# Layers 2 and 3 of a conv-attention kernel: from two streams ordered by a planner to four blocks in one written order

## The chip, the cores and the metric

The kernel runs on one core of one Trainium2 chip. The metric is the device time of one execution in microseconds (us). TensorE is called PE here (PEld is its weight loading), VectorE DVE, ScalarE ACT, GpSimd POOL and SyncE SP.

## The reference

An input of 8 images with 128 channels and 16x16 positions (256 tokens an image, 2048 in all) goes through four layers, all in float32:

- Layer 0: an "adder" convolution (sums of absolute differences) with residual.
- Layer 1: three selective scans (Mamba branches), a channel attention, two 3x3 convolutions.
- Layer 2: attention and a mixture of experts, for each image:
```python
x = x + softmax(LN(x Wq) @ LN(x Wk).T / sqrt(D)) @ (x Wv)      # x normed first
p = softmax(LN(x) @ router_w + router_b)                       # 8 experts, best 2 kept, renormed
x = x + sum_e p_e * (LN(x) @ expert_w[e] + expert_b[e])
```
- Layer 3: an encoder-decoder of eight Performer layers (linear attention over 8 heads with 44 random features), each followed by an MLP of 512 hidden units with GELU, and a bottleneck of 10 units after the fourth; then a spectral layer:
```python
h = LN(x) @ tok_W + pos
for i in range(8):
    u = LN(h); q, k, v = rotary(u Wq), rotary(u Wk), u Wv
    kf = exp(k F - |k|^2/2 - max) + eps; qf = exp(q F - |q|^2/2 - max) + eps
    h = h + (qf @ (kf.T @ v) / (qf @ sum(kf))) @ Wo
    h = h + gelu(LN(h) @ W1) @ W2
    if i == 3: h = gelu(h @ enc) @ dec
x = x + tanh(h);  out = x + spectral(LN(x))
```

## The kernel before

The 2048 tokens are four blocks of 512 columns (two images each); a block's activations are tiles of 128 channels by 512 tokens. Layers 0 and 1 and the spectral layer are not changed. `mamba_layer` (layer 1) ends with convolutions on PE, named `conv` in the profile; its last two pairs of images are finished there, so X of blocks 2 and 3 is ready last.

`performer_layer` holds layers 2 and 3. It makes two streams, `_performer_stream`, one for blocks 0 and 1 and one for blocks 2 and 3. Each stream has its own pools: `ptwo` (two buffers for each name), `pmany` (five buffers shared by short-lived tiles) and `pps`, four of the eight PSUM banks. Within a stream two blocks go side by side: `_norms` does both blocks' layer norms (`xc` on PE, square on ACT, `var` on PE, logarithm and exponential on ACT, `u` on DVE), `_layer2` the attention of each image (`_image`) and the experts, `_performer_attention` one Performer attention.

A stream is a generator that yields between parts; `interleave` takes one part of each stream in turn. That is the order in which the instructions are recorded, and not yet the order in which the engines run them: a planner with costs of its own then orders each engine's queue by priority and by when it thinks the inputs are ready. The first `HALF_LAYER` = 16 parts of the first stream are recorded with the priority of layer 1's last convolutions.

ACT needs its function table reloaded when it goes from exponentials and logarithms (`LN_EXP`) to GELU and tanh (`GELU`) or back; the class `Tables` holds the activations of each stretch of one stream between its two loads, and the two streams cross each other. Loads appear in the profile as `ACT_TABLE_LOAD`.

Weights of one Performer layer (`lw`, 948 KB) are loaded by SP in `_Layer`, with two buffers in the pool `plw`, one load for both streams; the first use of a layer makes it.

Names that the profile shows in one Performer layer, in the order of the computation: `xc`, `var`, `u` (norm); `pa`, `ro`, `rk`, `rq`, `sqk`, `sqq` (k and q with the rotation; `rk` and `rq` end on POOL); `pl`, `dt`, `dg` (squares by head, transposed); `pf`, `mxk`, `ek` (features of k, for each of four groups of 128 tokens); `m`, `pm`, `gm`, `dm`, `pg` (maximum over all tokens of an image); `pv`, `vo` (values); `pq`, `mq`, `ex`, `px`, `qp` (features of q, transposed); `pc`, `ctx`, `ks` (k by v); `pn`, `rd`, `po` (result, H); then `xc`, `var`, `u`, `p<-u,lw` and `g` (hidden units with GELU), `p<-g,lw` (back to 128), H. In layer 2 the router is `pl<-lw,u`, the routing a chain of small operations on the tile `ex`, and the experts `pe` on PE and `y` on DVE (line 1160), ended by `po2e`. The spectral layer begins with `p<-T,H`, which needs `pt` (line 1626) of its images.

Before the change the queues of PE, DVE, ACT and POOL in layer 1's scans are already written by hand with `tc.manual_schedule`, which makes the recorded order the order of those four engines.

Of the kernel before, what the change touches and what calls it, by code (L numbers as in the profile page):

```python
# [16 lines left out]
P = 128  # L17
# [248 lines left out]


class Tables:

    def __init__(self, E):
        self.E = E
        self.at = len(E.nc.cur_bb.bb.instructions)
        self.last = None

    def use(self, name):
        ins = self.E.nc.scalar.preload_act_table_set(name).ins
        traced = self.E.nc.cur_bb.bb.instructions
        for i in traced[self.at :]:  # L280
            if i is ins or i.engine != ins.engine:
                continue
            self._order(ins, i)
            if self.last is not None:
                self._order(i, self.last)
        if self.last is not None:
            self._order(ins, self.last)
        self.at, self.last = len(traced), ins

    def _order(self, late, early):  # L290
        info = mybir.DependencyInfo(mybir.DependencyClass.NoSync, mybir.DependencyReason.DATA)
        self.E.tc.add_manual_dep(late, early.name, info, reason="tables")
# [727 lines left out]

class _Layer2:
# [44 lines left out]

def _layer2(S, x):

    nc, two, many = S.nc, S.two, S.many
# [3 lines left out]
    us = yield from _norms(S, x)  # L1073
    qkv = []
    for u in us:
        xcs, rstds = [], []
        for n in ("q", "k"):
            xc = bank(S, [P, BLK], "xc2")
            S.mm(xc, w[n], u)
            sq = many.tile([P, BLK], F32, tag="t", name="lsq2")  # L1080
            nc.scalar.activation(sq, xc, AF.Square)
            xcs.append(xc)
            rstds.append(sq)
        yield True
        for sq in rstds:
            var = bank(S, [P, BLK], "var2")
            S.mm(var, S.mean, sq)
            nc.scalar.activation(sq, var, AF.Ln, bias=S.eps)
            nc.scalar.activation(sq, sq, AF.Exp, scale=-0.5)
        yield True  # L1090
        got = []
        for n, xc, rstd in zip(("q", "k"), xcs, rstds):
            d = two.tile([P, BLK], F32, tag="r" + n, name=n + "2")
            nc.vector.tensor_mul(d, xc, rstd)
            nc.vector.tensor_scalar(d, d, S.v(n + "n_w"), S.v(n + "n_b"), ALU.mult, ALU.add)
            got.append(d)
        v = two.tile([P, 4, P], F32, tag="vo", name="v2")
        pv = bank(S, [P, 4, P], "pv2")
        for c in range(4):
            S.mm(pv[:, c, :], u[:, c * P : (c + 1) * P], w["v"])  # L1100
        nc.scalar.copy(v, pv)
        qkv.append((*got, v))
        yield True

    for b in range(2):
        cols = slice(b * L, (b + 1) * L)
        parts = [
            _image(S, q[:, cols], k[:, cols], v[:, 2 * b : 2 * b + 2, :], xj[:, cols]) for (q, k, v), xj in zip(qkv, x)
        ]
        while parts:  # L1110
            parts = [p for p in parts if next(p, None)]
            yield True


    us = yield from _norms(S, x)
    room = two.tile([P, HM], F32, tag="ex0", name="ex2")
# [8 lines left out]
    g = 2 * BLK // P  # L1125
    pl = bank(S, [P, g, NE], "pl2")
    for j, u in enumerate(us):
        for c in range(4):
            S.mm(pl[:, 4 * j + c, :], u[:, c * P : (c + 1) * P], w["router"])
    p = take("p", [P, g, NE])  # L1130
    nc.vector.tensor_tensor(p, pl, bc(S.r("router_b"), 1, g), ALU.add)
    softmax_last(S, take, p, "sm")
# [13 lines left out]
    yield True  # L1146

    half = NE // 2
    for j, (u, xj) in enumerate(zip(us, x)):
        y = many.tile([P, 4, P], F32, tag="t", name="y2")  # L1150
        for c in range(4):
            for e0 in (0, half):
                pe = bank(S, [P, half, P], "pe2")
                S.mm(pe, u[:, c * P : (c + 1) * P], w["w"][:, e0 * P : (e0 + half) * P])
                for e in range(half):
                    weight = hot1[:, 4 * j + c, e0 + e : e0 + e + 1]
                    if e0 + e == 0:
                        nc.vector.tensor_scalar_mul(y[:, c, :], pe[:, e, :], weight)
                    else:
                        nc.vector.scalar_tensor_tensor(y[:, c, :], pe[:, e, :], weight, y[:, c, :], ALU.mult, ALU.add)  # L1160
            yield True
        pt = bank(S, [NE, 4, P], "pt2e")
        for c in range(4):
            nc.tensor.transpose(pt[:, c, :], hot1[:, 4 * j + c, :], ident)
        wt = many.tile([P, BLK], F32, tag="t", name="wt2")[0:NE]
        nc.scalar.copy(wt, pt.rearrange("e c n -> e (c n)"))
        po = bank(S, [P, BLK], "po2e")
        S.mm(po, w["b"][0:NE, :], wt, start=True, stop=False)
        for c in range(4):
            S.mm(po[:, c * P : (c + 1) * P], y[:, c, :], ident, start=False, stop=c == 3)  # L1170
        nc.vector.tensor_add(xj, xj, po)
        yield True


def _image(S, q, k, v, X):

    nc, two, many = S.nc, S.two, S.many
# [7 lines left out]
    yield True  # L1185
    at = two.tile([P, 2, L], F32, tag="ctx", name="at2")
    sm = two.tile([P, 2], F32, tag="sm2", name="sm2")
    for i in range(2):
        nc.scalar.activation(
            at[:, i, :], pa[:, i, :], AF.Exp, scale=scale, bias=mx[:, i : i + 1], accum_out=sm[:, i : i + 1]  # L1190
        )
# [3 lines left out]
    yield True  # L1195
# [6 lines left out]
    yield True  # L1202
# [4 lines left out]
    yield True  # L1207

def performer_layer(E, W):


    nc, tc = E.nc, E.tc
    with ExitStack() as ctx:
        S = Env.__new__(Env)
        S.__dict__.update(E.__dict__)
        T0, T1 = (Env.__new__(Env) for _ in range(2))

        def enter(name, bufs, **kw):  # L1220
            return ctx.enter_context(tc.tile_pool(name=name, bufs=bufs, reuse_waits="tile", **kw))

        def own(T, j):

            T.two = enter(f"ptwo{j}", 2)
            T.many = enter(f"pmany{j}", 5)
            T.psum = enter(f"pps{j}", 4, space=PSUM)

        own(T0, 0)
        S.small = one = enter("pone", 1)  # L1230
        S.lw = enter("plw", 2)
        own(T1, 1)
        S.tables = Tables(E)
        S.H, S.spectral = W.H, W
        S.keps = one.tile([P, 1], F32, tag="keps", name="keps")
        nc.gpsimd.memset(S.keps, KEPS)
        S.lb = one.tile([P, NL], F32, tag="lb", name="lb")
        for i in range(NL):
            nc.gpsimd.tensor_scalar_mul(S.lb[:, i : i + 1], S.v(f"ln1_b{i}"), float(L))
        S.layers = {"2": _Layer2(S)}  # L1240
        streams = []
        for j, T in enumerate((T0, T1)):
            T.__dict__.update({k: v for k, v in S.__dict__.items() if k not in T.__dict__})
            streams.append(_performer_stream(T, (2 * j, 2 * j + 1)))
        with tc.high_priority(offset=tc.cur_priority - E.mark):
            for _ in range(HALF_LAYER):
                next(streams[0])
        interleave(streams)

EXCHANGE = [i ^ 1 for i in range(32)]

HALF_LAYER = 16


def interleave(parts):

    while parts:
        parts = [p for p in parts if next(p, None)]  # L1260


def bank(S, shape, name):
    return S.psum.tile(shape, F32, tag="b", name=name)
# [25 lines left out]
def _norms(S, srcs, g=None, b=None, sums=None):  # L1290


    nc = S.nc
    xcs, rstds, out = [], [], []
    for src in srcs:
        xc = bank(S, [P, BLK], "xc3")
        S.mm(xc, S.center, src)
        sq = S.many.tile([P, BLK], F32, tag="t", name="lsq3")
        nc.scalar.activation(sq, xc, AF.Square)  # L1299
        xcs.append(xc)  # L1300
        rstds.append(sq)
    yield True
    for sq in rstds:
        var = bank(S, [P, BLK], "var3")
        S.mm(var, S.mean, sq)

        nc.scalar.activation(sq, var, AF.Ln, bias=S.eps)
        nc.scalar.activation(sq, sq, AF.Exp, scale=-0.5)
    yield True
    for j, (xc, rstd) in enumerate(zip(xcs, rstds)):  # L1310
        u = S.two.tile([P, BLK], F32, tag="u", name="u3")
        if sums is None:
            nc.vector.tensor_mul(u, xc, rstd)
        else:
            for q in range(2):
# [3 lines left out]
                )  # L1319
        if g is not None:  # L1320
            nc.vector.tensor_scalar(u, u, g, b, ALU.mult, ALU.add)  # L1321
        out.append(u)
    yield True
    return out

# [76 lines left out]
def _performer_attention(S, i, w, H, u, sums, j):  # L1402
# [129 lines left out]
    for b in range(2):  # L1532
# [10 lines left out]
        if b == 0:  # L1543
            yield True
# [222 lines left out]
```

## Time and profile before

| | us |
|---|---|
| median of 3 runs | 3185.14 |
| lowest to highest | 3185.01 to 3186.36 |
| the profiled execution's own time | 3185.76 |
| its span (first to last instruction) | 3184.0 |

| engine | busy us in the span | share |
|---|---|---|
| PE | 2947.6 | 93% |
| DVE | 2437.6 | 77% |
| ACT | 2204.9 | 69% |
| POOL | 732.8 | 23% |

The profile comes from one execution; times in it are us from the span's start, and a stretch A:B means that window. Layer 0 takes the first 950 us, layer 1 goes on to about 1836 us, layers 2 and 3 to 2946 us, and the spectral layer to the end at 3184 us. Rows of a group give busy time and mean duration; idle time is given with the instruction that ended it. A matmul in float32 is two records in the trace, a transpose one. The ends of matmuls are modelled, so the start-to-start distance in a dense run tells more of a matmul's cost than its record's length.

### The profile page before, as it was taken

How to read it: one execution, taken by the hardware profiler on the slowest of the kernel's cores; microseconds unless marked ns; L12 is line 12 of the kernel's file. 1: busy time of each engine (PE TensorE's matmuls, PEld its weight loads, DVE VectorE, ACT ScalarE, POOL GpSimd, SP SyncE). 2: the span in 40 equal slices, each digit the busy share in tenths (PEclk: the TensorE clock that was granted, in tenths of full speed). 3: DMA queues.
4: the chain of work that ended last, by engine and by line, in shares of the span. 5: the costliest groups of instructions: out<-in, count | busy, mean ns of one | idle time of the engine just before them, and what ended most of it. 6: DMA issues, size and time to landing. Idle time of an engine off the chain costs nothing.

```text
span 3184.0 us, 42472 instructions
## 1 busy us (share of the span) xinstructions
PE 2947.6 (93%) x16686; PEld 1299.8 (41%) x16686; DVE 2437.6 (77%) x3419; ACT 2204.9 (69%) x2653; POOL 732.8 (23%) x433
## 2 busy tenths in 40 slices
PE   6999999999997778998997988999999999999999
PEld 2333332333332223333433444555555555555444
DVE  6999999999996999999999257676576577574531
ACT  6999999999995887778776143666667766767111
POOL 3000000000001788778878000010010010010110
PEclk9999999999998999999999998999999999999999
DMA  1000000000001443443443000000000000001100
GB/s 38 1 1 5 1 1 5 1 1 5 1 1 47 166 147 127 146 142 127 151 141 125 17 27 13 1 13 1 13 13 1 13 13 1 13 1 37 53 27 14
DMA packets 39196, 131.47 MB, mean 41 GB/s; under 512 B 7490, under 2 KB 10572, under 8 KB 37588
## 3 DMA queue, kind: packets, MB, share of 16 engines
q1 hardware_dynamic: 38564, 128.02, 11.9%
q8 instruction: 132, 2.16, 0.3%
q10 hardware_dynamic: 432, 0.73, 0.1%
q14 instruction: 68, 0.56, 0.1%
HBM read 125.85 MB, written 1.84 MB: 40 GB/s over the span
## 4 chain that ended last, share of the span: by engine, by line
PE 65%; DVE 22%; ACT 6%; POOL 4%; issue 2%; DMA 1%; DVEq 0%; ACTq 0%; POOLq 0%; SPq 0%
PE o L265 30%; PE p L265 8%; DVE st L839 8%; DVE hc L848 4%; PE g L265 3%; PE pc L265 3%; PE conv L265 3%; PE acc L265 2%; PE pq L265 2%; PE xc L265 2%; PE var L265 2%; POOL dbu L753 2%; PE pv L265 1%; PE pn L265 1%; PE px L1521 1%
## 5 line engine op out<-in xcount | busy, mean ns | idle before, releaser
L265 PE MATMUL o<-d,sel 128*32 128x512 f32 x8800 | 946.4, 592 | 5.5 <-DVE d L432 5.5
L434 ACT ACTIVATE d<-sh,w 128x2048 f32<-128x2048 f32 x460 | 886.3, 1996 | 63.3 <-PE o L265 54.8
L432 DVE TENSOR_SCALAR d<-sh,w 128x2048 f32<-128x2048 f32 x640 | 789.4, 1291 | 47.5 <-PE o L265 39.8
L753 POOL TENSOR_TENSOR dbu<-du,bs 128x1024 f32<-128x1024 f32 x191 | 447.1, 2368 | 1019.4 <-DVE du L727 990.5
L265 PEld LDWEIGHTS o<-d,sel 128*32 128x32 f32 x8800 | 298.2, 110 | 653.0 <-issue 540.9
L839 DVE TENSOR_TENSOR_SCAN st<-da,dbu 128x512 f32<-128x512 f32 x384 | 447.9, 1207 | 13.3 <-POOL dbu L753 11.3
L265 PE MATMUL acc<-hc,cst 128*128 128x512 f32 x768 | 377.3, 616 | 84.8 <-DVE hc L848 84.3
L766 ACT ACTIVATE da<-delta,neg_a 128x510 f32<-128x510 f32 x384 | 256.6, 685 | 81.4 <-DVE st L839 80.4
L265 PEld LDWEIGHTS acc<-hc,cst 128*128 128x128 f32 x768 | 137.1, 192 | 293.4 <-DVE hc L848 173.1
L848 DVE TENSOR_TENSOR hc<-st,pcs 128x1024 f32<-128x1024 f32 x192 | 234.5, 1221 | 25.4 <-ACT tok L894 0.5
L1426 POOL TENSOR_TENSOR rk<-rk,ro 128x512 f32<-128x512 f32 x32 | 40.8, 1275 | 890.3 <-DVE rk L1422 620.5
L758 ACT COPY pcs<-cs 128x512 f32<-128x512 f32 x192 | 112.6, 586 | 79.9 <-DVE hc L848 78.5
L1699 ACT COPY ug<-p 128x512 f32<-128x512 f32 x64 | 37.5, 586 | 177.0 <-PE p L265 177.0
L265 PE MATMUL p<-u,lw 128*128 128x512 f32 x256 | 128.7, 621 | 15.2 <-DVE u L1321 13.3
L265 PE MATMUL conv<-pad,f 128*128 128x512 f32 x288 | 133.8, 598 | 3.2 <-ACT pad L994 2.1
L426 DVE SCALAR_TENSOR_TENSOR d<-sh,w,d 128x2048 f32<-128x2048 f32 x52 | 122.3, 2352 | 1.9
L265 PE MATMUL p<-T,H 128*128 128x512 f32 x256 | 115.6, 602 | 7.3 <-DVE ug L1701 6.3
L1471 ACT ACTIVATE ek<-ek 128x352 f32<-128x352 f32 x128 | 59.8, 492 | 88.0 <-DVE ek L1468 87.8
L1522 ACT ACTIVATE qp<-px,keps 88x512 f32<-88x512 f32 x128 | 84.2, 678 | 51.8 <-PE px L1521 51.2
L265 PE MATMUL p<-g,lw 128*128 128x512 f32 x256 | 114.6, 595 | 0.8 <-ACT g L1363 0.8
L265 PE MATMUL g<-ug,me 128*128 128x512 f32 (+1 forms) x320 | 112.0, 509 | 0.0
L1299 ACT ACTIVATE lsq<-xc 128x512 f32<-128x512 f32 x80 | 47.4, 596 | 76.3 <-PE xc L265 76.2
(322 smaller groups left out, 4064.0 us busy)
## 6 DMA issues: line engine op xcount, KB each, us to landing
bs<-rows SPq DMA_DIRECT2D x96, 512.0 KB, 3.9
cs<-rows SPq DMA_DIRECT2D x96, 512.0 KB, 4.8
m<-in_Mphi SPq DMA_DIRECT2D x8, 1024.0 KB, 4.9
lw<-in_layers SPq DMA_DIRECT2D x8, 948.0 KB, 4.6
f<-in_fuse SPq DMA_DIRECT2D x2, 1152.0 KB, 8.1
T<-in_T SPq DMA_DIRECT2D x1, 2064.0 KB, 8.1
x<-in_x SPq DMA_DIRECT2D x4, 256.0 KB, 6.2
total<-sums SPq DMA_DIRECT2D x16, 64.0 KB, 2.0
```

What stands on the lines that cost most here:

```text
L265: self.nc.tensor.matmul(out, lhsT=lhsT, rhs=rhs, start=start, stop=stop)
L426: nc.vector.scalar_tensor_tensor(held, tap(k), w[:, k, f : f + 1], held, ALU.max, ALU.add)
L432: nc.vector.tensor_scalar(d, tap(k), wk, None, ALU.max)
L434: nc.scalar.activation(d, tap(k), AF.Abs, scale=-1.0, bias=wk)
L753: gen.tensor_tensor(dbs[r], got[r // NST]["du"], bc(row("bs", r), 1, 2), ALU.mult)
L758: nc.scalar.copy(pcs[r], row("cs", r))
L766: nc.scalar.activation(das[g % 3][:, :, 1:], d[:, :, 1:], AF.Exp, scale=a)
L839: nc.vector.tensor_tensor_scan(st[:, h, :], da, dbs[r][:, h, :], 0.0, ALU.mult, ALU.add)
L848: nc.vector.tensor_tensor(hc, st, bc(pcs[r][:, :], 1, 2), ALU.mult)
L1299: nc.scalar.activation(sq, xc, AF.Square)
L1471: nc.scalar.activation(e, e, AF.Exp, scale=0.5)
L1522: nc.scalar.activation(qp[:, :, c * P : (c + 1) * P], px, AF.Identity, bias=S.keps[0:PAIR, :])
```

## The change

The two streams of two blocks become four blocks, each a generator `_block` of its own (`_norm`, `_layer2`, `_attention` for one block). Each block has its own pools: `pone` (one buffer for each name), `ptwo`, `pmany` (three buffers) and two PSUM banks. The generators yield more often: a block is 298 steps, most of which hold a short run of PE work and then what DVE, ACT and POOL do with it; a step's result is mostly used by PE only in a later step.

The first 30 steps of blocks 0 and 1, all of their layer 2, are recorded in turn (`AHEAD`) with the priority of layer 1's last convolutions and go to the planner as before. All other steps are recorded in the order of `ORDER`, a list of 1132 block numbers, under `tc.manual_schedule`, so PE, DVE, ACT and POOL each issue them in that order. SP (the loads) stays with the planner. Table loads are now put in by `act` and `tables` wherever the written order needs another table. Within a layer `pv` moves between `pm` and `pg`, the small operations on `sums` and `ub` move ahead of `pl`, and the routing is done for each block by itself, over 4 groups of tokens instead of 8. The numbers of the lines shift by some 25.

```diff
+        blocks = [Env.__new__(Env) for _ in range(NBLK)]
+        def own(t):
+            T = blocks[t]
+            T.t = t
+            T.one, T.two, T.many = enter(f"pone{t}", 1), enter(f"ptwo{t}", 2), enter(f"pmany{t}", 3)
+            T.psum = enter(f"pps{t}", 2, space=PSUM)
...
+        with tc.high_priority(offset=tc.cur_priority - E.mark):
+            for t in AHEAD:
+                next(steps[t])
+        with tc.manual_schedule(engines={nc.tensor.engine, nc.vector.engine, nc.scalar.engine, nc.gpsimd.engine}):
+            for t in ORDER:
+                next(steps[t], None)
...
-        with tc.high_priority(offset=tc.cur_priority - E.mark):
-            for _ in range(HALF_LAYER):
-                next(streams[0])
-        interleave(streams)
...
+AHEAD = [t for i in range(30) for t in range(2) if i < (30, 30)[t]]
+ORDER = [int(t) for t in (
+    "2312231312321312320312031032031203103230132103113211301320120032110321112331311010331033013310023123"
...
+def tables(S, name):
+    if S.table["now"] != name:
+        S.table["now"] = name
+        S.tc.keep_in_program_order(S.nc.scalar.preload_act_table_set(name))
+
+def act(S, out, src, func, **kw):
+    if func in (AF.Exp, AF.Ln):
+        tables(S, LN_EXP)
+    elif func in (AF.Gelu, AF.Tanh):
+        tables(S, GELU)
+    S.nc.scalar.activation(out, src, func, **kw)
...
+def _norm(S, src, g=None, b=None, sums=None):
+    nc = S.nc
+    xc = bank(S, [P, BLK], "xc3")
+    S.mm(xc, S.center, src)
+    sq = S.many.tile([P, BLK], F32, tag="t", name="lsq3")
+    act(S, sq, xc, AF.Square)
+    yield
+    var = bank(S, [P, BLK], "var3")
+    S.mm(var, S.mean, sq)
+    act(S, sq, var, AF.Ln, bias=S.eps)
+    act(S, sq, sq, AF.Exp, scale=-0.5)
+    yield
...
+def _block(S):
+    nc, one = S.nc, S.one
+    h, x = S.H[:, blk(S.t)], S.X[:, blk(S.t)]
+    yield from _layer2(S, x)
+    u = yield from _norm(S, x)
...
     for i in range(NL):
+        yield from _attention(S, i, h)
         w = _layer(S, i)
+        u = yield from _norm(S, h, S.v(f"ln2_g{i}"), S.v(f"ln2_b{i}"))
+        g = one.tile([P, 4, BLK], F32, tag="g", name="g3")
+        for f in range(0, 4, 2):
+            p1 = [bank(S, [P, BLK], "p1") for _ in range(2)]
+            for n in range(2):
+                S.mm(p1[n], w["w1"][:, (f + n) * P : (f + n + 1) * P], u)
+            for n in range(2):
+                act(S, g[:, f + n, :], p1[n], AF.Gelu, bias=S.v(f"b1{i}", f + n))
+            yield
...
-    g = 2 * BLK // P
+    g = BLK // P
     pl = bank(S, [P, g, NE], "pl2")
...
     dm = one.tile([2 * NH, 2 * NH], F32, tag="dm", name="dm")
     nc.vector.tensor_scalar_mul(dm, ident[0 : 2 * NH, 0 : 2 * NH], gm)
-    pg = bank(S, [P, 2, NH], "pg3")
-    S.mm(pg.rearrange("p b h -> p (b h)"), S.ones[0 : 2 * NH, :], dm)
...
     for c in range(4):
         S.mm(pv[:, c, :, :], u[:, c * P : (c + 1) * P], wv[:, :, 0:PD])
+    yield
+    pg = bank(S, [P, 2, NH], "pg3")
+    S.mm(pg.rearrange("p b h -> p (b h)"), S.ones[0 : 2 * NH, :], dm)
...
     for c in range(4):
-        yield True
         turned(c, ex[c])
+        yield
         if c + 2 < 4:
             ex.append(query(c + 2))
+            yield
```

## The prediction

> **What bounds the kernel now.** I read the page first, for the whole span:
> ```profile
> PE 2947.6 (93%) x16686; PEld 1299.8 (41%) x16686; DVE 2437.6 (77%) x3419; ACT 2204.9 (69%) x2653; POOL 732.8 (23%) x433
> ```
> The change touches only layers 2 and 3. The groups by line put the last `conv` before 1835.8 us and the last `pt` of line 1626 at 2946: 1110 us. I cut these into stretches (columns: bounds, length, busy us of PE, PEld, DVE, ACT, POOL with counts, granted clock, DMA share, GB/s):
> ```profile
> 1835.70:1872.00 36.30, 27.12 (x91) 15.12 (x92) 19.68 (x48) 19.92 (x42) 7.08 (x1) 0.91 0.16 58
> 1872.00:1915.00 43.00, 39.26 (x137) 21.67 (x136) 30.77 (x107) 18.93 (x39) 0.00 (x0) 0.96 0.00 1
> 1915.00:1989.00 74.00, 62.43 (x213) 29.85 (x211) 52.66 (x180) 23.51 (x48) 5.08 (x4) 0.89 0.04 14
> 1989.00:2289.00 300.00, 285.10 (x1598) 164.52 (x1598) 198.93 (x522) 197.42 (x323) 25.61 (x20) 0.98 0.02 7
> 2289.00:2589.00 300.00, 284.62 (x1603) 160.58 (x1602) 199.58 (x524) 201.50 (x323) 25.62 (x20) 0.99 0.02 7
> 2589.00:2889.00 300.00, 285.06 (x1595) 162.06 (x1594) 195.79 (x513) 204.88 (x329) 25.60 (x20) 0.99 0.02 7
> 2889.00:2946.00 57.00, 54.93 (x277) 30.07 (x276) 24.06 (x47) 39.29 (x59) 2.46 (x4) 1.00 0.14 51
> ```
> PE is the bound, with 72 us idle in 1110. DVE and ACT stand at about two thirds. But a matmul's record (592 ns for 512 columns) is longer than what it costs in a stream. The chain of waits shows that (start, us, group, records):
> ```profile
> 2116.83 6.87 PE p L265 x16
> 2103.03 2.37 PE pq L265 x8
> 2107.11 2.92 PE pc L265 x36
> 2114.76 0.45 PE px L1521 x4
> ```
> A record of 512 columns costs 0.429 us, of 352 columns 0.296, a `pc` about 0.08, a `px` 0.11. Each wait adds the idle time plus 592 − 429 = 0.16 us of drain that the page counts as busy.
>
> I add up PE's work by these prices. One block in one layer of layer 3 has 30 records of 512 columns (12.9 us), 16 of 352 (4.7), `pn` 2.1 (64 of them start within 4.27 us), `pc` 3.0, `px` 1.7, `pv`, `pl`, `pm`, `pg` 1.9: together 26.3. Thirty-two of these are 841 us. Layer 2 is 22 a block (88), and tokens, encoder and last norms 27. Sum: 956 us. The 18 `p<-T,H` that already run before 2946 are 15. So of 1110 us, 971 are work and **139 are lost**: 46 before 1989 and about 93 after it.
>
> Where they are lost, from the waits of PE in 1989 to 2889 (us in total, times, longest):
> ```profile
> PE p L265 <- DVE u L1321: 13.3, 6, 2.2
> PE pg L265 <- DVE dm L1483: 10.8, 16, 0.7
> PE pl L265 <- ACT sqq L1421: 6.1, 12, 0.6
> PE pl L1449 <- ACT dt L1447: 4.2, 10, 0.7
> PE p L265 <- ACT g L1363: 2.7, 13, 0.2
> PE pl L1449 <- DVE rq L1422: 2.3, 6, 0.4
> ```
> These are short chains, `pm`-`gm`-`dm`-`pg` for one, which PE reached with nothing else queued, and they recur in every layer. That is where a new order can help.
>
> **The change, part by part.** The built programs of both kernels have 8713 PE instructions of the same kinds and sizes. So 956 us of work stay, and the 139 us are all that can be won. The instructions up to the last `conv` are the same too, and so is the spectral layer.
>
> *Margins in the new order.* For every PE instruction that waits for DVE, ACT or POOL I compared two sums: the PE work that stands between the matmul that feeds the chain and the instruction, and the chain's durations from the rows of this trace. Before, 95 of 916 such waits have less work than chain, 46.6 us short in all, spread evenly (some 4.4 us in each 100). After, 59 of 819 are short by 20.0 us, 11.7 of it in the first 100 us of work. `pg` is no longer among them (`pv` now stands between `pm` and `pg`), and `dt` nearly not. So 29 us of certain waits go from the stretch after 1989. This counts each chain alone, with no queue before it, so it says nothing on the rest of the loss.
>
> *Margins that get thinner.* 272 of 819 waits have under 1 us to spare, against 257 of 916. All four engines now follow one interleaving of four blocks, so a late DVE or ACT instruction has every later step of all blocks behind it. Before, 154 PE starts were over 0.3 us late, 122 us in all, 0.79 each. Lower bound of this cost: zero, if thin margins hold. Upper bound: the rate of before, 154/257 late starts for each thin margin, gives 272 × 0.6 × 0.79 = 129 us, 7 more than before. I take 0: the 40 us or so that are late by queues after 1989 stay as they are.
>
> *Clock.* Granted 0.98, 0.99, 0.99 in the three stretches of 300 us is 12 us lost; half-speed windows of 3.4 us open within 4 us of the 2.2 us waits for `u` or of a run of `pg` waits. With these gone I take 8 of the 12 back (bounds 0 and 12).
> The Trainium skill (TensorE: Matmul & The Clock Gate, Part 1: The HAM clock gate) says half clock comes after about 3.4 us idle, which no wait here reaches, so by it these 8 us would not come and the forecast below would be 3156 instead of 3148.
>
> *Table loads.* The rows of `ACT_TABLE_LOAD` in this section hold 41 + 39 + 22 + 17 + 9 = 128 loads of 1.283 us:
> ```profile
> L278 ACT ACT_TABLE_LOAD x41 | 52.6, 1283 | 0.7
> L1363 ACT ACT_TABLE_LOAD x39 | 50.0, 1283 | 0.7
> ```
> The program goes from 131 to 136 loads: 6.4 us more on an ACT that is busy 705 of 1110 us, behind PE's work; without that cover, 6.4 us later.
> The Trainium skill (ScalarE: Activation LUTs, What ACT_TABLE_LOAD costs) adds a drain of 1.38 us to each switch, which would make these five 13 us; in this trace the next activation starts within 0.02 us of a load's end, so the row holds.
>
> *Start.* `AHEAD` now runs all of layer 2 for blocks 0 and 1 before blocks 2 and 3 do more than one `xc`. Before, their attention took until 1872 with the same two blocks; the norm, the routing and the experts were then mixed with blocks 2 and 3. Now they stand alone: norm 6, two routing chains 8 (one of 25 operations took 1884.2 to 1891.7; there are 98 small operations in place of 50, half as wide, and two chains fill each other's gaps), then 64 expert operations on DVE:
> ```profile
> 1892.77 3.70 DVE L1160 SCALAR_TENSOR_TENSOR y<-pe,ex,y 128x128 f32<-128x128 f32 x14
> ```
> 0.264 each, 17 us, and 3 for `po2e`. That ends at 1906 with 44 of the work done in 70 us: 26 lost. Afterwards blocks 2 and 3 do their layer 2 beside layer 3 of the others, where before 24 us were lost from 1915 to 1989; I take 14. So 40 against 46: 6 won (bounds −10 and +20).
>
> *End.* Before, `p<-T,H` filled the last steps of blocks 2 and 3, with 2 us idle after 2889. Now the four blocks end together, and only one `p<-T,H` stands among the last `pt`. The chain from the last `p` (0.75 H, 1.28 table, 0.63 tanh, 0.69 X, `xc` 0.86, square 0.60, `var` 0.86, table 1.28, 1.31, 0.69 u, `pt` 0.44) is 9 to 10 us with 4 to 5 of other PE work in it: 6 lost (bounds 0 and 10).
>
> *SP.* Layer weights are still two buffers deep. The nearest release of a buffer to its next use has 15.2 us of PE work between (layer 1), against 4.6 us from issue to landing: no wait.
>
> Sum: −29 −8 −6 +6 = −37 from the profiled 3185.76: 3148.8. The median of before is 0.6 lower, so **3148**. The forecast's own range, from 0 to all 12 of the clock and the bounds of start and end, is 3126 to 3172.
>
> **Rivals.** *One late engine stops all (slower).* The place is layer 3 with DVE, which holds `mq`, `ex`, `mxk`, `ek` (0.52 each) of four blocks in one queue. If lateness follows thin margins as above, big losses are 129 us, the small ones stay at 30, and the start (10) and the end (6) get worse, with the clock as it was: 175 against 122 + 27 = 149, so +26: 3212. It decides as soon as over 38 us are lost in each 300 us of layer 3, against 33 now. For it: DVE and ACT at 66%, and 165 places where a block takes two steps in a row. Against: the waits before are certain ones in large part.
>
> *Nearly full PE (faster).* Only the certain 20 us, 26 small bubbles under 0.3 us and 20 of lateness are left: 66 lost against 139: 3113. For it: 37 of the certain waits fall where they recur. Against: thin margins.
>
> *Stalls move, and nothing changes.* PE shows 95% busy, and each removed wait turns up at the next late chain: 3185. For it: the same work on three engines. Against: lateness of `u` (2.2 us each) has no successor in the margins.
>
> **How the numbers follow.** Forecast 0.50, nearly full 0.20, slower 0.20, no change 0.10. About 0.2% (6.4 us) is what a measurement of this kernel can tell. Faster: 0.50 + 0.20 + 0.03 of the no-change case = 0.73; same 0.06; slower 0.21. The range reaches below 3113 by the spread of that case and up into the slower rival: 3102 to 3204, with some 0.06 below and 0.12 above.
>
> **What would show it.** Right: in stretches of 300 us of layer 3 PE idle falls from 15 to under 10 and the clock is 1.00; `p` no longer waits for `u`, nor `pg` for `dm`; the stage is shorter by over 30 us while the counts of PE stay. Idle PE from 1872 to 1906 and some 6 us at the end would confirm these two prices. Wrong: PE waits behind `mq`, `ex` or `ek` of DVE, or ACT behind table loads, with DVE or ACT over 80% busy there.

## Result, and the profile after

The changed kernel takes 3228.47 us (median of 4 runs, 3226.15 to 3236.45) against 3185.07 us (4 runs) of the kernel before on the same chip: ratio 1.014, interval 1.0123 to 1.0158, so 43 us slower. The prediction of 3148 us was wrong, and its range ended at 3204. The profiled execution took 3226.15 us, its span 3224.3 us, 40.3 more than before. By the groups by line the last `pt` now comes at 2982.9 us instead of 2945.7: 37 of the 40 us are lost before that mark, in layers 2 and 3.

The page of the changed kernel, busy us, share and instructions of each engine:
```profile
PE 2958.1 (92%) x16686; PEld 1306.8 (41%) x16686; DVE 2517.3 (78%) x3467; ACT 2223.2 (69%) x2660; POOL 734.7 (23%) x433
```
PE's count is that of before, as foreseen. DVE has 48 more instructions and 79.7 us more busy time. Forty-eight small ones cannot make that, so some DVE instructions must have become longer.

The stretches (bounds, length, busy us of PE, PEld, DVE, ACT, POOL with counts, granted clock, DMA share, GB/s), the last one up to the new end of the section:
```profile
1835.70:1872.00 36.30, 29.19 (x96) 15.43 (x94) 19.48 (x45) 19.84 (x44) 7.08 (x1) 0.95 0.14 55
1872.00:1915.00 43.00, 36.62 (x97) 15.80 (x96) 27.33 (x120) 10.81 (x20) 0.00 (x0) 0.88 0.00 1
1915.00:1989.00 74.00, 63.70 (x311) 37.27 (x310) 62.18 (x175) 34.67 (x75) 5.22 (x4) 0.95 0.00 1
1989.00:2289.00 300.00, 276.06 (x1499) 155.11 (x1499) 217.69 (x529) 190.50 (x303) 24.11 (x19) 0.97 0.03 11
2289.00:2589.00 300.00, 272.04 (x1519) 155.16 (x1516) 207.94 (x493) 204.07 (x315) 24.09 (x19) 0.97 0.02 7
2589.00:2889.00 300.00, 275.43 (x1520) 158.05 (x1519) 216.32 (x510) 193.37 (x307) 25.37 (x20) 0.95 0.02 7
2889.00:2983.00 94.00, 89.24 (x462) 49.38 (x461) 50.64 (x108) 69.23 (x103) 4.96 (x6) 0.95 0.03 9
```
In the three stretches of 300 us PE's idle time rose from 45 to 76 us in all, and the clock fell to between 0.95 and 0.97. Priced as in the prediction, PE lost 35, 34 and 32 us there before and 43, 47 and 47 after. Yet no engine is full: DVE is busy 73, 69 and 72%.

The waits of PE in 1989 to 2889 (us in total, times, longest):
```profile
PE xc L265 <- DVE H L1346: 13.1, 7, 3.1
PE pl L265 <- ACT sqq L1079: 9.1, 8, 1.7
PE pg L265 <- DVE dm L1454: 9.1, 7, 2.6
PE pz L265 <- DVE H L1346: 8.2, 3, 4.3
PE pq L265 <- DVE ctx L1523: 7.0, 4, 2.9
...
PE p L265 <- DVE u L1158: 2.0, 3, 1.6
```
The largest wait of before, `p` for `u`, did go (13.3 to 2.0). In its place stand fewer and longer waits, most of them for results of DVE (`pz` is the first matmul of the bottleneck). So the question is what makes DVE late at 72% busy. Its own waits in the same window answer half of it:
```profile
DVE rk L1390 <- ACT sqk L1079: 31.2, 29, 3.0
DVE rq L1390 <- ACT sqq L1079: 27.7, 29, 1.7
```
Before, the same view held one such row, for `rq` alone:
```profile
DVE rq L1422 <- ACT sqq L1421: 7.0, 14, 0.7
```
59 us in place of 7. The groups of DVE hold the other half (busy us and mean ns of one, then idle time):
```profile
L1405 DVE TENSOR_SCALAR ub<-ones,us 128x88 f32<-128x88 f32 x64 | 46.7, 768 | 1.1
L1485 DVE TENSOR_TENSOR mq<-mq,dg 128x8 f32<-128x8 f32 x128 | 29.1, 227 | 4.4
```
Before, `ub` took 14.8 us and not 46.7:
```profile
L1456 DVE TENSOR_SCALAR ub<-ones,us 128x88 f32<-128x88 f32 x64 | 14.8, 258 | 0.3
```
One place in the timeline shows both (start, length, idle time before with its releaser; a row of x2 ends with its second instruction):
```profile
2220.60 0.69 ACT L1079 ACTIVATE sqq<-pa,vecs 128x512 f32<-128x512 f32 x1 [0.22 <-DVE ro L1386]
...
2221.32 0.75 DVE L1390 SCALAR_TENSOR_TENSOR rq<-pa,vecs,cst 128x512 f32<-128x512 f32 x1 [0.81 <-ACT sqq L1079]
...
2222.00 0.72 DVE L1392 STREAM_SHUFFLE ro<-ro 128x512 f32<-128x512 f32 x1
...
2222.62 0.27 DVE L1401 TENSOR_SCALAR us<-us,vecs,lb 128x2 f32<-128x2 f32 x1
2222.89 1.27 POOL L1394 TENSOR_TENSOR rq<-rq,ro 128x512 f32<-128x512 f32 x1 [12.01 <-DVE us L1401]
2222.93 1.48 DVE L1405 TENSOR_SCALAR ub<-ones,us 128x88 f32<-128x88 f32 x2
...
2224.33 0.68 DVE L1150 TENSOR_TENSOR u<-xc,lsq 128x512 f32<-128x512 f32 x1
```
First, `ro`, the square and `rq` read the same bank `pa` one after the other: ACT's square starts when DVE is through with `ro`, and `rq` starts 0.03 us after the square ends. DVE stands still for 0.81 us although the shuffle of `ro` (0.72 us) could run. (Why `rq`, which takes nothing from the square, waits for it, no run here tests.) Second, the two `ub` start 0.04 us after POOL's addition and end just after it, 1.48 us instead of some 0.5. Behind both stands everything else DVE has to do, here `u` of another block, which PE waits for.

### The profile page after: what moved, and what is told of

Its sections match the earlier page's. It is cut to its first block, busy times and chain, and to the rows that moved or that the text cites. A ratio compares the mean times of both kernels' runs of the same rounds, so it can differ in the third digit from the quotient of the medians.

```text
span 3224.3 us, 42449 instructions
## 1 busy us (share of the span) xinstructions
PE 2958.1 (92%) x16686; PEld 1306.8 (41%) x16686; DVE 2517.3 (78%) x3467; ACT 2223.2 (69%) x2660; POOL 734.7 (23%) x433
## 4 chain that ended last, share of the span: by engine, by line
PE 58%; DVE 25%; ACT 10%; POOL 4%; issue 2%; DMA 1%; DVEq 0%; ACTq 0%; POOLq 0%
PE o L265 29%; DVE st L812 8%; PE p L265 5%; DVE hc L821 4%; PE g L265 4%; PE conv L265 3%; ACT L1071 2%; PE acc L265 2%; PE xc L265 2%; POOL dbu L726 1%; PE var L265 1%; PE pn L265 1%; ACT g L1079 1%; PE pf L265 1%; PE pq L265 1%
## 5 line engine op out<-in xcount | busy, mean ns | idle before, releaser
L1071 ACT ACT_TABLE_LOAD x134 | 171.9, 1283 | 2.4
L1079 ACT ACTIVATE ex<-ex 128x352 f32<-128x352 f32 x128 | 62.9, 494 | 109.2 <-DVE ex L1487 104.5
```

The source lines that it names most:

```text
L1071: S.tc.keep_in_program_order(S.nc.scalar.preload_act_table_set(name))
L1079: S.nc.scalar.activation(out, src, func, **kw)
```

## The experiments

The expectations call the second place theory A or A2 (`ub` beside the rotation's addition) and, from e9 on, the first place theory D (DVE at the head of its fixed queue, waiting for the square); in e5 and e8 the letter D stands for something else. Each names its rivals itself. All times are medians, with the ratio to the kernel before. The sums' operations "back" means behind `dg`'s copy, as before the change. The runs that are not in the table (e2, e4, e5, e8, e12, e14) change something else and stand in the text alone.

| kernel | engines in the written order | sums | shuffle | us | ratio |
|---|---|---|---|---|---|
| changed kernel | PE, DVE, ACT, POOL | early | behind `rk`, `rq` | 3228.5 | 1.014 |
| e13 | all four | early | ahead | 3175.5 | 0.9968 |
| e1 | all four | back | behind | 3182.8 | 0.9993 |
| e9 | all four | back | ahead | 3144.9 | 0.9879 |
| e10 | PE, ACT, POOL | early | behind | 3134.2 | 0.9843 |
| e7 | PE, ACT, POOL | back | behind | 3134.0 | 0.9846 |
| e15 | PE, ACT | back | behind | 3133.9 | 0.9838 |
| e6 | ACT | back | behind | 3125.2 | 0.9815 |
| e11 | ACT | back | ahead | 3127.3 | 0.9821 |
| e3 | none | early | behind | 3159.0 | 0.992 |

### The sums' operations moved back (e1)
```diff
     q, sqq = rotated("q")
-    nc.vector.tensor_scalar(sums, sums, ...)
-    ub = one.tile([P, 2, PAIR], F32, tag="ub", name="ub3")
-    for b in range(2):
-        nc.vector.tensor_scalar(ub[:, b, :], ...)
     yield
...
     nc.vector.tensor_copy(dg.rearrange(...), pl[:, :, 0 : 2 * NH])
+    nc.vector.tensor_scalar(sums, sums, ...)
+    ub = one.tile([P, 2, PAIR], F32, tag="ub", name="ub3")
+    for b in range(2):
+        nc.vector.tensor_scalar(ub[:, b, :], ...)
     yield
```


> The changed kernel with the three small operations on sums and ub moved back behind the copy of dg, one step later; the written order of the blocks is the same. Theory A (the two ub operations stand right behind the start of POOL's addition on rq and wait for its end, 32 times about 1.0 us of DVE, and everything behind them in the written order is late): ub falls from 0.77 to 0.26 us, DVE's busy time by some 33 us, and the time by 20 to 33 us, to 3195 to 3208. Theory B (the order's margins are too thin for queues that run late for any reason; ub is only one of them): ub falls as well, but the time by at most 10 us, to 3218 or more. Theory C (one buffer for each name and two PSUM banks for each block make engines wait for buffers): no change, 3226 to 3230.

Measured 3182.78 us (10 runs), ratio 0.9993 (0.9984 to 1.0003): 46 us less than the changed kernel, the whole of its loss. The group of `ub` in this kernel:
```profile
L1425 DVE TENSOR_SCALAR ub<-ones,us 128x88 f32<-128x88 f32 x64 | 14.1, 263 | 1.1
```
`ub` takes 32.6 us less and DVE as a whole 23 us less (`mq` now meets POOL's addition more often, 280 ns for 227); the time fell by more than either. The wait of `rk` and `rq` for the square is still there:
```profile
DVE rk L1390 <- ACT sqk L1079: 32.9, 30, 3.0
DVE rq L1390 <- ACT sqq L1079: 29.2, 30, 1.7
```

### `ub` made by ACT (e2)
```diff
-        nc.vector.tensor_scalar(ub[:, b, :], S.ones[:, 0:PAIR], sums[:, b : b + 1], KEPS, ...)
+        act(S, ub[:, b, :], S.kones, AF.Copy, scale=sums[:, b : b + 1])
```


> The changed kernel with ub made by ACT (64 copies with a scale, some 0.25 us each, 16 us on an ACT that is busy 69%) at its place in the written order; the small operation on sums stays on DVE. Theory A: DVE loses 64 times 0.77 = 49 us of busy time, and the time falls by 30 to 45 us, to 3183 to 3198, more than with the operations moved back. Theory B: under 15 us, 3213 or more. Theory C: no change.

Measured 3229.62 us, ratio 1.0141 (1.0124 to 1.0158): no gain, against the expectation. DVE no longer has the long `ub`, but the wait moved to ACT's queue, which is fixed as well. ACT's waits in 1989 to 2889:
```profile
ACT ub L1081 <- DVE us L1403: 47.4, 29, 1.7
```
It stands 1.6 us each time for an operation that nobody needs soon. DVE has 37 us less to do, and the time is the same: in a fixed queue the place costs on ACT as it did on DVE. That it is this wait which takes the gain back is read from the row; no run takes it away.

### The addition on DVE (e4)
```diff
-        nc.gpsimd.tensor_add(r, r, o)
+        nc.vector.tensor_add(r, r, o)
```


> The changed kernel with the addition that ends the rotation on DVE and not on POOL, 64 of some 0.69 us: 44 us more work on DVE, nothing left on POOL in layer 3 that could hold DVE up (41 us of waiting on ub and the mq and ctx operations gone). Theory A: DVE's sum is the same to within 5 us, but the chain from the shuffle to pf is shorter by 0.6 us, so 3205 to 3230. Theory B (DVE's length in the order counts, not who is waited for): the same or slower, 3225 to 3260.

Measured 3215.29 us, ratio 1.0094 (1.0079 to 1.0109). With nothing on POOL beside them `ub` takes 262 ns instead of 768, `mq` (line 1485) 167 instead of 227, the second `ctx` 414 instead of 537:
```profile
L1405 DVE TENSOR_SCALAR ub<-ones,us 128x88 f32<-128x88 f32 x64 | 14.1, 262 | 1.1
L1485 DVE TENSOR_TENSOR mq<-mq,dg 128x8 f32<-128x8 f32 x128 | 21.4, 167 | 4.4
```
These three are 44 us less on DVE, all its groups together 49, and the 64 additions (692 ns) bring 44 us, so the sum says 5 us; 13 came. That POOL's addition is what stretched these is shown; as a remedy it gives most of it back.

### `ub` left out (e5)
The two operations on `sums` and `ub` are left out, and `ub` is a constant tile.
```diff
-    ub = one.tile([P, 2, PAIR], F32, tag="ub", name="ub3")
-    ...
+    ub = S.ubc
```


> The changed kernel without the operations on sums and ub at all (the term of ub is a constant, so that part of the computation is left out; everything else and the written order are the same). Theory A2 (the operations stand in front of other blocks' work in DVE's written order while POOL holds them, and that alone made the change slower): the time is that with the operations moved back less their 32 x 0.27 + 64 x 0.26 = 25 us of DVE at most, 3155 to 3183. Theory D (something else in the written order was upset, and moving the operations back changed it by luck): 3190 or more.

Measured 3171.9 us, ratio 0.9962 (0.9947 to 0.9977): 57 us less than the changed kernel, 11 less than with the operations moved back. Moving them is therefore worth four fifths of what leaving them out is.

### The kernel before with the operations early (e8)
```diff
     q, sqq = rotated("q")
+    ub = two.tile([P, 2, PAIR], F32, tag="ub", name="ub3")
+    nc.vector.tensor_scalar(sums, sums, ...)
+    for b in range(2): ...
     yield True
```


> The kernel before, with the three operations on sums and ub recorded right behind the rotation of q, as the changed kernel has them; the planner orders all engines. Theory A2: ub is long here as well where the planner leaves it beside POOL's addition (0.5 us or more), but DVE has only two thirds of its time taken and the planner's queue is not led by one order for all, so 3185 to 3200. Theory D: no change, 3180 to 3187.

Measured 3186.23 us, ratio 1.001 (1.0001 to 1.0019). The same early place in the recorded order costs 3 us where the planner orders DVE and 46 us where the order is fixed. The stall itself is smaller here, though: the planner leaves only a part of the `ub` beside POOL's additions, and it takes 371 ns in the mean (258 before, 768 in the changed kernel), less than the 0.5 us expected.

### Who writes the order (e3, e6, e7)
In e3 the steps are recorded in the written order, but the planner orders all engines; in e6, with the sums back, ACT alone; in e7, with the sums back, all but DVE.
```diff
-        with tc.manual_schedule(engines={nc.tensor.engine, nc.vector.engine, nc.scalar.engine, nc.gpsimd.engine}):
+        if True:                                                                                    # e3
+        with tc.manual_schedule(engines={nc.scalar.engine}):                                        # e6
+        with tc.manual_schedule(engines={nc.tensor.engine, nc.scalar.engine, nc.gpsimd.engine}):    # e7
```


> The changed kernel recorded step by step in the same order, but with the planner ordering the queues of the four engines, as in the kernel before. Theory B: the planner moves late instructions out of the way, and the time falls to that of before or below, 3160 to 3190. Theory A: it falls only as far as the planner happens to separate ub from POOL's additions, by 0 to 33 us. Theory C: the buffers are the same, so it stays at 3220 or more.

Measured 3158.95 us, ratio 0.992 (0.9905 to 0.9935), although the planner's ACT needs 227 table loads on lines 1071 and 1079 where the written one needs 134 (119 us more of ACT). So the four blocks with their own buffers and two banks each are not what costs: in an order made by readiness they gain some 25 us.

> The operations on sums and ub moved back, and only ACT issues in the written order (134 table loads); PE, DVE and POOL are ordered by the planner. Theory B2 (after ub is moved, what is lost in layer 3 is lost by the written order on PE and DVE, where a late instruction holds back work that is ready): faster than the planner on all four engines with its 227 table loads, 3125 to 3155. Theory E (the planner gained by free choice on ACT as well): 3155 to 3185.

Measured 3125.21 us, ratio 0.9815 (0.98 to 0.9829), the fastest kernel of this study: 59 us below before by its ratio, 57 us below e1, from which it differs in the order of PE, DVE and POOL alone. Its three stretches of 300 us:
```profile
1989.00:2289.00 300.00, 293.19 (x1649) 165.88 (x1647) 216.54 (x589) 205.63 (x333) 28.11 (x22) 1.00 0.03 11
2289.00:2589.00 300.00, 296.96 (x1695) 167.15 (x1694) 213.30 (x556) 222.37 (x349) 26.69 (x21) 1.00 0.03 11
2589.00:2889.00 300.00, 293.60 (x1640) 165.58 (x1640) 198.26 (x491) 221.06 (x346) 24.14 (x21) 1.00 0.03 12
```
PE's idle time is 16 us where the changed kernel has 76, and the clock is full. DVE is nearly as busy as in the changed kernel (628 us in all against 642), only in another order. The last stretch holds the first 4 to 5 us of the spectral layer. Against e3 the place of the sums differs too, but with DVE free that place costs nothing that shows (e10 and e7 below), which leaves ACT's order, with its fewer loads, for most of the 34 us between them.

> The operations on sums and ub moved back; PE, ACT and POOL issue in the written order, DVE is ordered by the planner. Theory B2 with DVE as the engine whose fixed order costs: half or more of the step from the written order to the planner, 3150 to 3168. If PE's own fixed order costs: no change against the written order with the operations moved back, 3176 to 3186. A planner that does not know the written order of the others could also make it slower.

Measured 3133.99 us, ratio 0.9846 (0.9829 to 0.9862). Against e1 only DVE's order is free: 49 us. DVE's waits for the square are 4.5 + 9.2 us in this trace, where e1 has 62.

### The shuffle ahead of the cosine product (e9)
```diff
-        nc.vector.scalar_tensor_tensor(r, pa, bias, bc(S.c("cos"), 1, 2), ALU.add, ALU.mult)
         o = o.rearrange("p b l -> p (b l)")
         nc.vector.stream_shuffle(o, o, EXCHANGE)
+        nc.vector.scalar_tensor_tensor(r, pa, bias, bc(S.c("cos"), 1, 2), ALU.add, ALU.mult)
```


> The kernel with the sums' operations moved back (3182.8 us) and one further exchange in VectorE's written order: in `rotated` the stream shuffle of `ro` stands ahead of the cosine product `rk`/`rq`, which waits for ScalarE's square of the same bank. Theory D (VectorE stands at the head of its fixed queue for that square: 32.9 + 29.2 us of waits between 1989 and 2889 us with the sums moved back, against about 13 us where the planner orders VectorE): the shuffle (0.4 to 0.5 us) covers most of each wait of about 1 us, the two waits fall from 62 us to under 25 us, and the time to 3145-3165 us. Rival E (what the written order loses on VectorE is the order between blocks, not this place in one step): the two waits fall, but others rise by as much and the time stays 3178-3186 us.

Measured 3144.93 us, ratio 0.9879 (0.9864 to 0.9893): 38 us less than e1, at the lower end of what theory D gave (its shuffle of 0.4 to 0.5 us was too short: the 64 take 0.73 us each in this trace). DVE's waits in 1989 to 2889:
```profile
DVE rq L1392 <- ACT sqq L1079: 11.2, 12, 1.4
DVE rk L1392 <- ACT sqk L1079: 9.8, 9, 2.2
```
62 us became 21. Two other waits of DVE grew, `u` (line 1150) for `lsq` from 12.9 to 26.1 us and H for `p` from 20.8 to 25.9, by 18 of these 41 us; so the rival has something in it, but the time fell by 38 us all the same, and PE's idle time in the three stretches from 56 us in e1 to 36.

### The shuffle alone (e13)
The edit of e9, made in the changed kernel with its sums early.

> The changed kernel with only the stream shuffle ahead of the cosine product; the sums' operations stay early. If the two places on VectorE's queue each make the steps behind them late by their own amount, the gain found with the sums moved back (3182.8 to 3144.9 us, 38 us) holds here too: 3228.5 - 38 = 3190 us, 3182-3200 us, with `ub` still at 750 to 790 ns. Rival (the queue has one slack that the first stall uses up; the second costs nothing beside it): 3212-3230 us.

Measured 3175.49 us (7 runs, 3168.88 to 3179.83), ratio 0.9968 (0.9957 to 0.998): 53 us less, more than either theory gave. `ub` is still long (754 ns). So each place alone gives back 46 or 53 us, and both together 84, not 99: they overlap by some 15 us, and the one does not hide the other.

### DVE free, with the sums early (e10)
The edit of e7, made in the changed kernel.

> The changed kernel with its early sums' operations kept, but VectorE left to the planner; TensorE, ScalarE and GpSimd in the written order. Theory A+D (a long `ub` beside the rotation's addition costs the path only where VectorE cannot take another ready operation first): 3132-3146 us, as with the sums moved back (3134.0 us). Rival (the blocked port costs the path by itself, whatever the order): 3160-3182 us, as the two written orders differ by 45 us.

Measured 3134.19 us, ratio 0.9843 (0.9828 to 0.9858), equal to e7. With DVE free, neither the early sums nor the order in `rotated` cost anything that shows. Its `ub` takes 289 ns: the planner issued it apart from POOL's additions (at 2220.47 us, for instance, with the next addition at 2225.64).

### The kernel before with the shuffle ahead (e14)


> The kernel before with the same exchange of shuffle and cosine product in its `rotated`. Its VectorE is ordered by the planner, which has rq wait 7.8 us and rk 0.5 us for the square in its whole section. Theory D: no gain to be had, 3178-3190 us. Rival (the exchange shortens the chain of each block and helps any order): 3145-3165 us.

Measured 3185.78 us, ratio 1.0 (0.999 to 1.0009): no gain. The exchange is worth 38 to 53 us in the fixed order, and nothing where the planner orders DVE (e11 says the same).

### Steps strictly in turn (e12)
```diff
-ORDER = [int(t) for t in (...)]
+ORDER = [t for i in range(298) for t in (2, 3, 0, 1)]
```


> The sums moved back and all four engines in a written order, but the steps of the four blocks taken strictly in turn (2, 3, 0, 1) in place of the written list. If the loss on VectorE comes from any fixed order with these waits in it (theory D), the time is near that of the list: 3170-3215 us, with the same waits of `rk` and `rq` for ScalarE of about 60 us. If the list itself is what costs (rival E: its phases put the blocks' waits together), the time falls to 3140-3165 us.

Measured 3376.82 us, ratio 1.0602 (1.0584 to 1.0619): both theories missed. The waits of DVE for the square are 12.0 + 20.5 us, and one row has grown, from 20.8 us in e1:
```profile
DVE H L1333 <- PE p L265: 138.2, 23, 14.9
```
With the sums back, the list of the change is 194 us better than plain turns, though it needs 98 table loads more (134 against 36). That two places inside its steps, and not the list, cost the change its gain is shown by e9, not here; some 11 us remain between e9 and e7, where DVE's order is free.

### ACT alone, with the shuffle ahead (e11), and PE's queue (e15)


> The fastest kernel so far (sums moved back, ScalarE alone in the written order, 3125.2 us) with the stream shuffle ahead of the cosine product. Theory D: the planner already fills these waits with other blocks' work (rk 3.5 us, rq 8.1 us left), so at most 10 us of waits can go and little of it is on the path: 3117-3127 us. Rival: the planner's own choice was fitted to the old place, and a block's chain becomes longer or shorter by the shuffle: below 3115 or above 3133 us.

Measured 3127.33 us, ratio 0.9821 (0.9806 to 0.9836): within 2 us of e6, whose planner had already filled these waits.

```diff
+        with tc.manual_schedule(engines={nc.scalar.engine, nc.tensor.engine}):
```


> The sums moved back, with ScalarE and TensorE in the written order and VectorE and GpSimd left to the planner. ScalarE alone in the written order gave 3125.2 us, and TensorE, ScalarE and GpSimd together 3134.0 us. If the written order costs TensorE nothing: 3123-3129 us. If the 9 us between them are TensorE's: 3131-3138 us.

Measured 3133.88 us, ratio 0.9838 (0.9823 to 0.9853): the 9 us between e6 and e7 are those of PE's written order, and POOL's costs nothing that shows. The waits of PE that are longer than in e6 are `pg` for `dm` (5.4 us against 1.2), `p` for `u` (4.7 against 0.8) and `pa` for `u` (3.9 against none listed).

## Why the prediction was wrong, point by point

*The failed step* is "Margins that get thinner", where the text says "I take 0", with an upper bound of 7 us. By the same prices the loss in the three stretches rose from 101 to 137 us, and the cause is DVE's fixed queue: with the other three engines in the same written order and DVE alone set free (e10), the changed kernel takes 94 us less. The margins set PE's work against the durations of one chain at a time, in the words of the prediction "with no queue before it", and the bound carried over 0.6 late starts for each thin margin from a trace whose DVE was ordered by readiness. In the fixed order that rate did not hold: a wait of 1 us in the middle of a step, harmless where DVE can take another block's work (e14, e11), makes every step of all four blocks late (e9, e13). The text said this in one clause ("a late DVE or ACT instruction has every later step of all blocks behind it") and gave it no price. A price could be had: 64 rotations with a square of 0.69 us between two products of DVE are 44 us. The waits measured are 59 us, and taking most of them away gave 38 to 53 us.

*An edit without a term.* The move of `sums` and `ub` ahead of `pl` is nowhere in the sum, so it stood at nothing without a reason. It lengthened 64 operations by 0.5 us and cost 46 us (31 once the shuffle stands ahead, e13 against e9). The trace of before already had the sign: `us`, 537 ns in the mean, has 283 in the median and 985 at most, and its long ones end with POOL's addition:
```profile
L1454 DVE TENSOR_SCALAR us<-us,vecs,lb x32: 276/283/985, 1957.6 to 2850.7; 128x2 f32<-128x2 f32 x32
```
The Trainium skill (SBUF — State Buffer, SBUF: two separate sides) says that GpSimd and some DVE instructions (those in a two-port mode or with two inputs in SBUF) share one pair of ports as an exclusive lock, held for a whole instruction while the other blocks. The timeline above agrees (`ub` ends 0.25 us after the addition), and so does e4 (262 ns with no addition on POOL).

*Certain waits, −29.* The sum of the six waits that the prediction showed fell from 39 us to 25; but others came (`xc` for H from 1.6 to 13.1). With DVE free and PE in the written order (e15) `pg` for `dm` is 5.4, `pl` for `sqq` 1.3, `p` for `u` 4.7 us, against 10.8, 6.1 and 13.3 before; with PE's order free too (e6) they are 1.2, 1.0 and 0.8. So the written order removes over half of these waits once DVE is not late, and the planner's order of PE most of the rest.

*Clock, −8.* It fell instead, to 0.95–0.97. In e6, where no wait of PE in 1989 to 2889 is over 1.5 us, it is 1.00 in all three stretches: the 12 us were to be had with shorter waits, as the prediction said.

*Start and end.* Up to 1915 us 25 us were lost, where 26 were foreseen up to 1906, and 18 up to 1989 instead of 14: 43 us in all against 46 before, so the start is some 3 us better, not 6. The end lost 11 us against 3, +8 for +6 foreseen.

*Table loads.* 134 loads on line 1071, 171.9 us, for 128 in the section before; the price of a load held:
```profile
L1071 ACT ACT_TABLE_LOAD x134 | 171.9, 1283 | 2.4
```
*SP.* No engine waited for a load of `lw` between 1836 and 2983 us.

*Two sums that do not come out.* The 18 `p<-T,H` are 18 records, two to a matmul, so they are 8 us and not 15. The loss before the change is then 146 us and not 139, which agrees with the 149 used for the slower rival, and the faster rival would stand some 7 us lower than 3113. And from the bounds as they are written (clock 0 to 12, start −10 to +20, end 0 to 10) the forecast's own range is 3134 to 3186, not 3126 to 3172. Neither would have put 3228 inside.

*The rivals.* "One late engine stops all" came true, in layer 3 and on DVE, with over 38 us lost in each 300 as its point; it gave 3212, 16 too few, and named `mq` and `ex` where it was `rk`, `rq` and `ub`. The sign set for it, DVE or ACT over 80% busy, did not show: here a fixed queue is late at 69 to 73%. Its size came from a rate of lateness for each thin margin, which is not what the runs showed, so its nearness to the result is in part luck. "Nearly full PE", 3113, is what e6 comes near with 3125, but with only one of the four queues fixed. And e9, which mends the two places and keeps all four written queues, takes 3144.9: a gain of the forecast's size was in this order, and two places in one engine's queue took it away. That e9 lands within 4 us of 3148 does not prove the sum: in e9 the six waits fell from 39 to 16 us, near the 29 foreseen, but the clock of the three stretches gave back 3 us and not 8.

What stays open: why the shuffle's place is worth 53 us with the sums early (e13) and 38 with the sums back (e9), and where the 11 us between e9 and e7 are lost.

## What to carry to other kernels

When an engine's order becomes fixed, go through that engine's queue step by step and price every wait inside a step as time for all that stands behind it; busy shares and single chains do not show it. Put an operation that is ready between one that feeds another engine and one that waits for that engine, and keep a small operation that nobody needs soon from standing right behind the start of a long instruction that can hold it up, here POOL's addition. Where an order is needed for one reason only, here the table loads on ACT, try fixing that queue alone: e6 was 20 us faster than the best kernel here with all four fixed.

## What the runs showed of the hardware

While POOL adds two SBUF tiles (1.27 us), several of DVE's small operations on SBUF tiles last until the addition is done: in e9 one `mq` of 8 columns (line 1485) takes 168 ns in the median and 1008 at most, and the long ones end 0.02 to 0.03 us behind an addition. An operation with an input in PSUM is not stretched: `ek` (line 1437) starts during an addition 10 times in that kernel and takes 523 to 526 ns in all 128 cases.
```profile
L1485 DVE TENSOR_TENSOR mq<-mq,dg x128: 166/168/1008, 1955.1 to 2862.0; 128x8 f32<-128x8 f32 x128
L1437 DVE TENSOR_TENSOR ek<-pf,mxk x128: 523/524/526, 1941.6 to 2840.8; 128x352 f32<-128x352 f32 x128
```
Nor is the shuffle of `ro`, although it reads and writes SBUF alone: 0.72 to 0.73 us in the four cases that start beside an addition. The 128x512 addition itself takes 1.27 us on POOL and 0.69 on DVE (e4).

The Trainium skill (TensorE: Matmul & The Clock Gate, Part 1: The HAM clock gate) gives half clock after about 3.4 us of idle. In e1 the longest wait of PE between 1989 and 2889 us is 2.7 us, and yet the clock granted there is 0.98 to 0.99. Cut into windows of 1 us, that part of the trace has six stretches at 0.50, four of them some 3.4 us long, one 7 and one 10. Five of the six begin within 0.8 us of the end of a single wait of 1.5 to 2.7 us, such as this one (the matmul behind the wait, then two windows with the granted clock as the third number from the end):
```profile
2292.56 0.39 PE L265 MATMUL pg<-dm,ones 16*128 16x16 f32 x2 [2.75 <-DVE dm L1454]
2292.00:2293.00 1.00, 0.44 (x3) 0.41 (x4) 1.00 (x2) 0.00 (x0) 0.48 (x1) 1.00 0.00 0
2294.00:2295.00 1.00, 1.00 (x2) 0.38 (x2) 1.00 (x3) 0.00 (x0) 0.00 (x0) 0.50 0.00 0
```
So in this kernel waits well under 3.4 us were enough to lose some of the clock. What decides it no run here shows.
